# Outlook attention on one core: each landed band of coefficients is copied into pairs of heads before the banded matmuls

## The chip, the core and the metric

The kernel runs on one core of a Trainium2 chip. A core has a matrix engine (TensorE, PE in the profile, with its weight loads as PEld), a vector engine (VectorE, DVE), a scalar engine (ScalarE, ACT), GpSimd (POOL) and SyncE (SP), whose queue issues most of the DMAs. The engines run on their own and wait for one another through semaphores. The metric is the time of one execution on the device in microseconds; a kernel is run three times or more and the median is given. A profile is one further execution, recorded by the hardware.

## What is computed

The whole program is a two-layer network over x of shape 4 x 32 x 32 x 384: an attention, a mixture of experts, an outlook attention and a factored two-layer net, each added to x. The change lies in the outlook attention, whose reference is:

```python
def _L1_conv_ref(x, Wv, Wa, Wo):
    HEADS, K, PAD = (12, 3, 1)
    v = jnp.einsum('bhwc,oc->bhwo', x, Wv)
    ...
    v_unf = patches.reshape(b, n, k2, heads, d)
    a = jnp.einsum('bhwc,oc->bhwo', x, Wa).reshape(b, n, heads, k2, k2)
    attn = jax.nn.softmax(a * d ** (-0.5), axis=-1)
    out = jnp.einsum('bnhpq,bnqhd->bnphd', attn, v_unf).reshape(b, h, w, k2, c)
    ...
    for i in range(k):
        for j in range(k):
            canvas = canvas.at[:, i:i + h, j:j + w].add(out[:, :, :, p])
            p += 1
    y = canvas[:, pad:pad + h, pad:pad + w]
    return jnp.einsum('bhwc,oc->bhwo', y, Wo)
...
x = x + _L1_conv_ref(_ln_c(x), L1_conv_Wv, L1_conv_Wa, L1_conv_Wo)
```

Each pixel has, for each of 12 heads, a 9 x 9 matrix of softmax weights. It mixes the nine values around the pixel into nine outputs, which are added onto the nine pixels around it. Put together, an output pixel is a weighted sum over the values of a 5 x 5 neighbourhood, with one coefficient (a sum of softmax weights) per head and offset. In the order of rows of 32 pixels, those offsets reach 66 pixels back and forth.

## The kernel before

**Tiling.** The 4 images of 1024 pixels are 32 tiles of 128 pixels, eight to an image (`NB = 8`); a tile's number is `o = b * NB + t`. Everything is float32. All of the outlook layer is in the function `outlook` (L1764); it runs from about 2265 to 2730 us of the span, between the experts (`experts`) and the factored net (`Kron.run`).

**What is done for a tile.** Five functions, each called once a tile or half image:

- `scores(b, t)` (L1852): normalizes the tile (`xn`), transposes it on TensorE (`ps_tr`) and copies the result to `xnT` (ScalarE, L156), computes the logits `ps_a` with twelve matmul records (L1862, two PSUM banks, one buffer), takes maximum, difference (VectorE, L1871 and L1872), exponential (ScalarE, L1877), sums and the division (VectorE, L1879 to L1886), and sends rows of the result to neighbouring partitions by DMA into `up` and `down` (SP queue, L1898 to L1903). It then computes the values `ps_v` (L1906) and copies them to `v` (ScalarE, L1910).
- `band(b, t)` (L1912): adds up the shifted pieces in `u` (two ScalarE copies, L1919 and L1920, and three VectorE additions), shifts sideways with matmuls (`ps_c`, L1927), masks into `co` (L1935), and writes `co` to a DRAM buffer `room` (SP queue, L1942). The write has one row of 5 x 60 coefficients per pixel and the rows lie skewed, so that reading the buffer back with another row length (L1948) gives the tile `band` of 128 partitions x `BAND` = 260 columns x 12 heads: for each of 128 input pixels, the coefficients to the 260 output pixels around, and zeros between. This is one DMA of 1560 KB.
- `gather(b, half, t)` (L1953): the banded matmuls. For each head `h` it multiplies the 128 x 32 values of the head with the 128 x n coefficients of the head (n = 260, or 194 or 66 where the band is cut at the edge of a half image of 512 pixels), and adds into `ps_y`. Four heads lie side by side in four column tiles (32 output partitions each), so the twelve heads are three groups `c` of four. In the trace a float32 matmul leaves two records, so a gather has 24. Tiles 3 and 4 of an image are gathered twice, once for each half. After the last tile of a half, ScalarE copies the three banks to `y` (L1973).
- `mix(b, half, n, y)` (L1976): the output projection `ps_wo` (L1980) and the addition to x (L1984).
- `add(i)` (L1831): for the first 15 or so steps, adds experts' results (gathered by GpSimd's indirect DMA into `yt`) to tiles that later steps need.

**The coefficients of one head** are read by the matmul as `bands[b, t][:, j : j + hi - lo, h]`: in memory the 12 heads of a column lie next to each other, so consecutive columns of one head lie 12 floats apart.

**What sets the order.** A loop of steps (L2018) calls `scores` for tile `step`, then the functions that were put down for this step with `at`: `band` two steps after its tile's scores, `gathered` `LAG` = 3 steps after that, `mixed` later. SyncE and GpSimd issue in this written order (`manual_schedule`, L2279). For TensorE, VectorE and ScalarE the framework's list scheduler orders the instructions at build, by the written order as priority and by when it reckons operands and buffers to be ready; on the chip each engine then keeps that order. A pool with `bufs=n` gives n buffers to a tag, and a new tile waits until the instructions that use the old one are done. `reuse_waits="tile"` tells the framework to keep such waits by the tile.

Of the kernel before, what the change touches and what calls it, by code (L numbers as in the profile page):

```python
# [10 lines left out]
FP = mybir.dt.float32  # L11
# [6 lines left out]
P = 128  # L18
# [5 lines left out]
NH, HD = 12, 32  # L24
# [18 lines left out]
BAND = P + 2 * REACH  # L43
# [1720 lines left out]
def outlook(net, wv, wa, wo, left, router, kron, loads):  # L1764
# [10 lines left out]
    tc, nc = net.tc, net.nc  # L1775
    K2, H6 = 9, NH // 2
# [3 lines left out]
    with ExitStack() as ctx:  # L1780
# [2 lines left out]
        mp = ctx.enter_context(tc.tile_pool(name="ol_moved", bufs=4, reuse_waits="tile"))  # L1783
        ap_ = ctx.enter_context(tc.tile_pool(name="ol_attn", bufs=3, reuse_waits="tile"))
        vp = ctx.enter_context(tc.tile_pool(name="ol_v", bufs=7, reuse_waits="tile"))
        bp = ctx.enter_context(tc.tile_pool(name="ol_band", bufs=5, reuse_waits="tile"))
        ps_m = ctx.enter_context(tc.tile_pool(name="ol_ps_m", bufs=2, space=PSUM, reuse_waits="tile"))
        ps_a = ctx.enter_context(tc.tile_pool(name="ol_ps_a", bufs=1, space=PSUM, reuse_waits="tile"))
        ps_c = ctx.enter_context(tc.tile_pool(name="ol_ps_c", bufs=1, space=PSUM, reuse_waits="tile"))
# [4 lines left out]
        for dx in (-1, 0, 1):  # L1794
            m = const.tile([P, P], FP, name=f"shift_{dx}", tag=f"shift_{dx}")
# [41 lines left out]
                )  # L1837
            net.measure(work, i, net.x(i))

        attn, vs, bands, ys, moved = {}, {}, {}, {}, {}  # L1840

        def room(b, t):

# [68 lines left out]
        def band(b, t):  # L1912


            H3 = 3 * H6
            u = work.tile([P, 6, 5, H3], FP, name="u", tag="u")
            down, up = (m.rearrange("p (g y e) -> p g y e", g=6, y=3) for m in moved.pop((b, t)))
            own = attn.pop((b, t))[:, 1].rearrange("p s x (y e) -> p (s x) y e", y=3)
            nc.scalar.copy(u[:, :, 0, :], down[:, :, 0, :])  # L1919
            nc.scalar.copy(u[:, :, 4, :], up[:, :, 2, :])  # L1920
            nc.vector.tensor_tensor(u[:, :, 1:3, :], down[:, :, 1:3, :], own[:, :, 0:2, :], ALU.add)
            nc.vector.tensor_tensor(u[:, :, 3, :], own[:, :, 2, :], up[:, :, 1, :], ALU.add)
            nc.vector.tensor_tensor(u[:, :, 2, :], u[:, :, 2, :], up[:, :, 0, :], ALU.add)
            pc = ps_c.tile([P, 512], FP, name="ps_c", tag="c")
            grid = pc[:, : 5 * R].rearrange("p (s y e) -> p s y e", s=2, y=5)
            for qj in (1, 0, 2):
                nc.tensor.matmul(  # L1927
                    grid[:, :, :, (2 - qj) * H6 : (5 - qj) * H6],
                    lhsT=shift[qj - 1],
                    rhs=u.rearrange("p (s x) y e -> p s x y e", s=2)[:, :, qj, :, :],  # L1930
                    start=qj == 1, stop=qj == 2, skip_group_check=True,
                )
            co = work.tile([P, 5, 5, NH], FP, name="co", tag="co", bufs=3)
            for hh in range(2):
                nc.vector.tensor_tensor(  # L1935
                    co[:, :, :, hh * H6 : (hh + 1) * H6],
                    grid[:, hh].rearrange("p y (x h) -> p y x h", x=5),
                    inside.rearrange("p (x h) -> p x h", x=5).unsqueeze(1).to_broadcast([P, 5, 5, H6]),
                    ALU.mult,
                )  # L1940
            room = net.room[t]
            nc.sync.dma_start(  # L1942
                out=room.rearrange("(p r) -> p r", p=P)[:, : 5 * IMG * NH]
                .rearrange("p (y r) -> p y r", y=5)[:, :, :R],
                in_=co.rearrange("p y x h -> p y (x h)"),
            )
            m = bands[b, t] = bp.tile([P, BAND, NH], FP, name="band", tag="band")
            nc.sync.dma_start(  # L1948
                out=m.rearrange("p t h -> p (t h)"),
                in_=room[: P * BAND * NH].rearrange("(p r) -> p r", p=P),  # L1950
            )

        def gather(b, half, t):  # L1953

            first, last = (0, 4) if half == 0 else (3, 7)
            lo = max(P * t - REACH, 512 * half)
            hi = min(P * t - REACH + BAND, 512 * half + 512)
            j = lo - (P * t - REACH)
            for c in range(KC):
                if t == first:  # L1960
                    ys[c] = ps_y.tile([P, 512], FP, name=f"ps_y{c}", tag=f"y{c}")
                for n in range(4):
                    h = 4 * c + n
                    nc.tensor.matmul(  # L1964
                        ys[c][32 * n : 32 * n + 32, lo - 512 * half : hi - 512 * half],
                        lhsT=vs[b, t][:, h * HD : (h + 1) * HD],
                        rhs=bands[b, t][:, j : j + hi - lo, h],
                        start=t == first, stop=t == last, skip_group_check=True,
                    )
            if t == last:  # L1970
                y = work.tile([P, KC, 512], FP, name="y", tag="y", bufs=1)
                for c in range(KC):
                    nc.scalar.copy(y[:, c, :], ys[c])  # L1973
                return y
# [14 lines left out]
        def at(step, f, *args):  # L1989
            later.setdefault(step, []).append((f, args))  # L1990

        LAG = 3
        made = {}

        def gathered(b, half, t):
            y = gather(b, half, t)
            if y is not None:
                made[b, half] = y
# [4 lines left out]
        for b in range(B):  # L2003
            for t in range(NB):
                o = b * NB + t
                at(o + 2, band, b, t)
                at(o + 2 + LAG, gathered, b, 0 if t < 5 else 1, t)
                if t == 4:
                    at(o + 2 + LAG, gathered, b, 1, 3)
                    at(o + 2 + LAG, gathered, b, 1, 4)  # L2010
            for half in range(2):
                done = b * NB + (4 if half == 0 else 7) + 2 + LAG
                for n in range(4):
                    at(done + 1 + n // 2, mixed, b, half, n)
        assert left[0] >= 2 * NB
        t_kron, first = 0, left[0]
        for step in range(B * NB + 9):
            b, t = divmod(step, NB)  # L2018
# [207 lines left out]
def metaformer_kernel(  # L2226
# [19 lines left out]
    def rest(router, done):  # L2246

        with ExitStack() as late:
# [30 lines left out]
            with tc.manual_schedule(engines={eng.SP, eng.Pool}):  # L2279
                outlook(net, wv, wa, wo, range(done, NT), router, kron, loads)  # L2280
# [85 lines left out]
```

## Time and profile before

The median of three runs is 2829.91 us (2828.95 to 2830.11). The profiled execution took 2827.02 us, of which the recorded span is 2825.3 us; the mean granted TensorE clock was 0.959.

| engine | busy us | share of the span | instructions |
|---|---|---|---|
| PE | 2615.5 | 93% | 14703 |
| PEld | 1570.2 | 56% | 14703 |
| DVE | 1720.6 | 61% | 4382 |
| ACT | 1203.6 | 43% | 2023 |
| POOL | 413.8 | 15% | 501 |

The page cuts the span into 40 equal slices of 70.6 us; a digit is the busy share in tenths:

```profile
PE   6889998999999997687999999999999988999988
DVE  1377777677778787657245444655555566877742
ACT  3778777678768876312222212112112122122225
PEclk9999999999999998789999999999999999999999
```

The outlook layer lies in slices 33 to 39 (the last eight digits but one): TensorE at eight or nine tenths, VectorE between four and eight, ScalarE at one or two. The page's list of the costliest groups has few lines of this layer, ps_a (L1862, 384 records, 169.5 us busy) at their head; the layer's other matmuls are found by asking for the groups of that stretch alone. A busy time of a group is the time in which at least one of its records runs: four matmuls in four column tiles run side by side, so the busy time of `ps_y` is far below its count times its mean duration. A wait is put down to whatever came last by the profile.

Among the DMA issues of the stretch from 2260 to 2760 us are 32 of `band<-room` (1560 KB), 32 of `room<-co` (150 KB), 60 of `up<-attn` and 60 of `down<-attn`, and early in it the loads of x for the later images (two of 1536 KB, one of 1344 KB). They share one queue.

### The profile page before, as it was taken

The numbers are of one execution on the slowest core, as the hardware profiler recorded it, in microseconds if no ns is written. First come the engines' busy times: TensorE is split into PE (matmuls) and PEld (weight loads), VectorE is DVE, ScalarE is ACT, GpSimd is POOL, SyncE is SP. The second block draws the span as 40 slices with busy tenths as digits, with TensorE's granted clock in tenths as the row PEclk, the third lists the DMA queues.
The fourth block names the chain that finished last, engine by engine and source line by source line (L and its number), as shares of the span: only waits on it lengthen the run. The fifth ranks groups of instructions, "written<-read, shape, count | busy, mean of one in ns | idle before, by whom it ended". The sixth has DMA issues, their size and how long they took to land. (4 is left out here: it accounts for less than half of the span.)

```text
span 2825.3 us, 40024 instructions
## 1 busy us (share of the span) xinstructions
PE 2615.5 (93%) x14703; PEld 1570.2 (56%) x14703; DVE 1720.6 (61%) x4382; ACT 1203.6 (43%) x2023; POOL 413.8 (15%) x501
## 2 busy tenths in 40 slices
PE   6889998999999997687999999999999988999988
PEld 3323333333333332167899999999999944444432
DVE  1377777677778787657245444655555566877742
ACT  3778777678768876312222212112112122122225
POOL 1000000030003003213211112222221101100000
PEclk9999999999999998789999999999999999999999
DMA  5143434222323242453655455565665447554432
GB/s 106 31 106 90 110 92 129 75 66 72 90 60 75 68 108 58 125 204 125 248 229 208 167 208 209 210 230 210 217 224 203 156 148 217 173 178 149 147 109 91
DMA packets 215804, 404.11 MB, mean 143 GB/s; under 512 B 83344, under 2 KB 176848, under 8 KB 202544
## 3 DMA queue, kind: packets, MB, share of 16 engines
q1 hardware_dynamic: 184496, 187.82, 22.3%
q0 software_dynamic: 26960, 209.05, 21.5%
q10 hardware_dynamic: 4144, 4.61, 0.5%
q8 instruction: 118, 1.93, 0.3%
q14 instruction: 86, 0.70, 0.1%
HBM read 304.34 MB, written 49.00 MB: 125 GB/s over the span
## 5 line engine op out<-in xcount | busy, mean ns | idle before, releaser
L1698 ACT ACTIVATE h<-ps_h,up 128x256 f32<-128x256 f32 (+1 forms) x420 | 195.1, 465 | 839.7 <-PE ps_h L1693 838.8
L1693 PE MATMUL ps_h<-xbT,up 128*128 128x256 f32 (+1 forms) x2520 | 531.8, 372 | 2.5 <-ACT h L1698 1.8
L689 DVE CUSTOM_DVE_ANT_0 e<-e,rz,inv 128x1024 f32<-128x1024 f32 x384 | 475.2, 1274 | 44.6 <-DMA rz<-r_row 44.3
L1693 PEld LDWEIGHTS ps_h<-xbT,up 128*128 128x128 f32 x2520 | 463.1, 191 | 64.5 <-ACT h L1698 2.6
L637 ACT ACTIVATE e<-ps_s,ten 128x1024 f32<-128x1024 f32 x384 | 408.1, 1110 | 64.8 <-PE ps_s L627 33.1
L627 PE MATMUL ps_s<-q,k 32*128 32x512 f32 x1536 | 295.2, 673 | 44.7 <-ACT e L637 31.4
L645 PE MATMUL ps_o<-e,wv 128*32 128x512 f32 x1536 | 226.1, 663 | 50.9 <-DVE wv L696 49.4
L1735 PE MATMUL ps_y<-wsum,hsum 128*128 128x192 f32 x1152 | 205.4, 332 | 22.8 <-DVE hsum L1656 19.6
L645 PE MATMUL ps_z<-e,rt_ones 128*32 128x512 f32 x1536 | 218.3, 642 | 0.0
L716 POOL DMA_DIRECT2D q<-po x96 | 76.1, 877 | 951.5 <-DMA q<-po 560.9
L373 ACT ACTIVATE below<-tk_left,tk_bound 128x1024 bf16<-128x1024 f32 (+1 forms) x160 | 184.4, 1152 | 52.6 <-DVE tk_bound L379 40.4
L1735 PEld LDWEIGHTS ps_y<-wsum,hsum 128*128 128x128 f32 x1152 | 190.9, 193 | 27.3 <-DVE hsum L1656 21.3
L627 PEld LDWEIGHTS ps_s<-q,k 32*128 32x128 f32 x1536 | 92.5, 193 | 182.2 <-ACT e L637 90.2
L1862 PE MATMUL ps_a<-wa,xnT 128*128 128x486 f32 x384 | 169.5, 589 | 9.2 <-DVE attn L1872 7.5
L1739 DVE TENSOR_TENSOR y<-ps_y,y 128x192 f32<-128x192 f32 x160 | 57.2, 357 | 172.0 <-PE ps_y L1735 168.8
L645 PEld LDWEIGHTS ps_o<-e,wv 128*32 128x32 f32 x1536 | 31.4, 112 | 212.5 <-DVE wv L696 64.5
L288 PE MATMUL ps_t<-xnT,wqkv 128*128 128x512 f32 x288 | 135.1, 609 | 2.4 <-ACT xnT L470 1.7
L1735 PE MATMUL ps_y<-down,h 128*128 128x192 f32 x768 | 130.0, 326 | 0.0
L1735 PEld LDWEIGHTS ps_y<-down,h 128*128 128x128 f32 x768 | 126.6, 190 | 1.9
L1862 PEld LDWEIGHTS ps_a<-wa,xnT 128*128 128x128 f32 x384 | 72.3, 194 | 95.2 <-issue 85.5
L645 PEld LDWEIGHTS ps_z<-e,rt_ones 128*32 128x32 f32 x1536 | 52.2, 117 | 131.0 <-issue 127.5
L1540 POOL DMA_INDIRECT yt<-yg,index x64 | 76.7, 1198 | 323.0 <-DVE x L1835 135.3
(392 smaller groups left out, 3539.2 us busy)
## 6 DMA issues: line engine op xcount, KB each, us to landing
band<-room SPq DMA_DIRECT2D x32, 1560.0 KB
rz<-r_row SPq DMA_DIRECT2D x48, 512.0 KB
yg<-y SPq DMA_DIRECT2D x67, 192.0 KB
q<-q SPq DMA_DIRECT2D x192, 64.0 KB
k<-k SPq DMA_DIRECT2D x192, 64.0 KB
room<-none SPq DMA_DIRECT2D x64, 192.0 KB
x<-x SPq DMA_DIRECT2D x35, 192.0 KB
o<-in_x_dram SPq DMA_DIRECT2D x33, 192.0 KB
```

The costliest lines, as they stand in the source:

```text
L288: nc.tensor.matmul(ps, lhsT=lhsT(k), rhs=rhs(k), start=k == 0, stop=k == KC - 1)
L373: nc.scalar.activation(junk[:n], left[:n], AF.Sign, bias=bound[:n], accum_out=over[:n])
L627: nc.tensor.matmul(ps[:, half * 512 : half * 512 + 512], lhsT=self.k4[r, u * P : (u + 1) * P], rhs=self.q4[r, :], start=True, stop=True,)
L637: nc.scalar.activation(e, ps, AF.Exp, bias=shift, scale=QK_SCALE)
L645: nc.tensor.matmul(ps[r : r + 32, :], lhsT=lhsT(odd), rhs=self.es[2 * u + odd][:, half * 512 : half * 512 + 512], start=u == 0, stop=u == ...
L689: nc.vector.tensor_tensor_reduce(self.es[m], self.es[m], self.rz, 1.0, self.im["inv"][:, m, self.h : self.h + 1], ALU.mult, ALU.add, self. ...
L716: nc.gpsimd.dma_start(out=there, in_=po[r : r + 32, :], accum_op=ALU.add)
L1540: self.nc.gpsimd.indirect_dma_start(out=y, out_offset=None, in_=self.net.yg[: first_row(self.complete(i // NB)), :], in_offset=bass.Indire ...
L1693: nc.tensor.matmul(ps, lhsT=up[:, o : o + P], rhs=xbT[:, k, :size], start=k == 0, stop=k == KC - 1,)
L1698: nc.scalar.activation(hs[f // 3][:, f % 3, :size], ps, AF.Gelu, bias=up[:, KC * HID + f : KC * HID + f + 1])
L1735: nc.tensor.matmul(ps, lhsT=left[f], rhs=right[:, f, :], start=f == 0, stop=f == HF - 1)
L1862: nc.tensor.matmul(pa[:, hh, :HW_], lhsT=xnT[:, k, :], rhs=wa[:, k, hh * HW_ : (hh + 1) * HW_], start=k == 0, stop=k == KC - 1,)
```

## The change

The landed band isn't read by the matmuls any more. A new function `sort`, called one step before the gather of its tile, copies it with six ScalarE copies, one for each pair of heads, from the order (column, head) into a new tile `own` of the order (pair of heads, column, head of the pair). The matmul reads `own` with the head's pair and its place in it: consecutive columns of one head now lie 2 floats apart. The five buffers of `band` become three for the landed bands and two for `own`, of the same size each.

```diff
-        bp = ctx.enter_context(tc.tile_pool(name="ol_band", bufs=5, reuse_waits="tile"))
+        bp = ctx.enter_context(tc.tile_pool(name="ol_band", bufs=1, reuse_waits="tile"))
...
-        attn, vs, bands, ys, moved = {}, {}, {}, {}, {}
+        attn, vs, landed, bands, ys, moved = {}, {}, {}, {}, {}, {}
...
-            m = bands[b, t] = bp.tile([P, BAND, NH], FP, name="band", tag="band")
+            m = landed[b, t] = bp.tile([P, BAND, NH], FP, name="band", tag="band", bufs=3)
             nc.sync.dma_start(
                 out=m.rearrange("p t h -> p (t h)"),
                 in_=room[: P * BAND * NH].rearrange("(p r) -> p r", p=P),
             )
+
+        def sort(b, t):
+
+            m = landed.pop((b, t)).rearrange("p t (n h) -> p n t h", h=2)
+            own = bands[b, t] = bp.tile([P, H6, BAND, 2], FP, name="own", tag="own", bufs=2)
+            for n in range(H6):
+                nc.scalar.copy(own[:, n], m[:, n])
...
-                        rhs=bands[b, t][:, j : j + hi - lo, h],
+                        rhs=bands[b, t][:, h // 2, j : j + hi - lo, h % 2],
...
                 at(o + 2, band, b, t)
+                at(o + 1 + LAG, sort, b, t)
                 at(o + 2 + LAG, gathered, b, 0 if t < 5 else 1, t)
```

In the list of a step, the entries stand by tile: the gather of tile `step - 5` first, then `sort` of tile `step - 4`, then `band` of tile `step - 2`.

## The prediction

> **What bounds the kernel now.** I read the page first (the row of busy tenths shows TensorE at nine tenths in slices 35 to 38), then the busy time of each engine stage by stage, then the groups of one stage by shape, then waits and order of time. The stage that the change touches runs from about 2265 to 2730 us of the span. By stretches:
>
> ```profile
> core 0: us, PE busy (x) PEld busy (x) DVE busy (x) ACT busy (x) POOL busy (x), PEclk, DMA share, GB/s
> 2320.00:2345.00 25.00, 24.38 (x103) 11.34 (x103) 17.07 (x42) 4.82 (x12) 2.49 (x3) 0.94 0.75 244
> 2345.00:2420.00 75.00, 64.30 (x310) 30.93 (x309) 53.49 (x138) 13.84 (x27) 14.81 (x15) 0.91 0.61 187
> 2420.00:2690.00 270.00, 268.79 (x1221) 132.44 (x1220) 198.05 (x502) 61.46 (x121) 12.05 (x15) 1.00 0.50 163
> 2710.00:2730.00 20.00, 12.34 (x83) 4.44 (x82) 3.89 (x10) 3.04 (x4) 0.00 (x0) 0.83 0.48 169
> ```
>
> In 2420 to 2690 TensorE is busy 268.8 of 270 us, VectorE 73%, ScalarE 23%; and what TensorE waited for there adds up to 1.2 us:
>
> ```profile
> PE ps_a L1862 <- ACT xnT L156: 0.6, 1, 0.6
> PE ps_c L1927 <- DVE u L1923: 0.4, 1, 0.4
> PE ps_a L1862 <- DVE attn L1872: 0.2, 1, 0.2
> ```
>
> So TensorE alone bounds these 270 us at full granted clock. Before 2420 it idles 14% behind other waits (DMA landings); after 2710 a chain of DMAs ends last. The banded matmuls there (each a pair of records, four column tiles side by side, so mean durations overlap; busy time is what counts):
>
> ```profile
> L1964 PE MATMUL ps_y<-band,v 128*32 128x260 f32 x226 | 35.5, 627 | 0.0
> L1964 PE MATMUL ps_y<-band,v 128*32 128x194 f32 x240 | 26.4, 515 | 0.0
> L1964 PE MATMUL ps_y<-band,v 128*32 128x66 f32 x96 | 3.6, 295 | 0.0
> ```
>
> 65.5 us, a quarter of the stage.
>
> **Edit 1: the matmul's moving operand (L1967) goes from a step of 12 floats (48 bytes) to 2 floats (8 bytes).** Start to start is the true pace, since ends are modelled. In order of time:
>
> ```profile
> 517.55 1.07 PE L645 MATMUL ps_o<-e,wv 128*32 128x512 f32 x8
> 518.43 1.04 PE L645 MATMUL ps_z<-e,rt_ones 128*32 128x512 f32 x8
> ...
> 2428.20 2.22 PE L1964 MATMUL ps_y<-band,v 128*32 128x194 f32 x24
> 2430.35 0.91 PE L1906 MATMUL ps_v<-wv,xnT 128*128 128x384 f32 x2
> ...
> 2458.15 2.90 PE L1964 MATMUL ps_y<-band,v 128*32 128x260 f32 x24
> 2460.99 0.55 PE L155 MATMUL ps_tr<-ident,xn 128*128 128x128 f32 x3
> ```
>
> 24 records are three groups of four heads, two passes each: six passes. 260 columns: 2.84/6 = 0.473 us a pass; 194 columns: 2.15/6 = 0.358 us. The slope is 0.115/66 = 1.74 ns a column, the rest 0.02 us; 66 columns (0.82/6 = 0.137 us) lie on the same line. The attention's ps_o runs in the same four column tiles, with contiguous operands: 0.88 us for two passes of 512, 0.86 ns a column. So four tiles side by side are not what costs; the step is, by a factor of 2.0.
>
> No matmul of this trace steps by 8 bytes, so its price lies between 0.86 and 1.74 ns. [...] That saves 48%, 48% and 44%: of 35.5, 26.4 and 3.6 us **17.1 + 12.6 + 1.6 = 31 us** in the bound stage. From 2320 to 2420 the same matmuls are 20.8 us busy and lose 10, but TensorE isn't alone in setting the time there: I count 3.
>
> **Edit 2: `sort`, six ScalarE copies a band, 6 x 32 = 192**, each 128x520, read in runs of two floats 48 bytes apart, written contiguously. Rows of ScalarE:
>
> ```profile
> L1877 ACT ACTIVATE attn<-attn 128x972 f32<-128x972 f32 x20 | 20.3, 1015 | 12.1 <-DVE attn L1872 12.1
> L1920 ACT COPY u<-up 128x108 f32<-128x108 f32 x21 | 6.0, 284 | 9.8 <-DMA up<-attn 9.7
> ...
> 2697.16 1.56 ACT L1973 COPY y<-ps_y 128x512 f32<-128x512 f32 x3 [3.72 <-PE ps_y L1964]
> ```
>
> Between 108 and 972 elements the slope is 0.85 ns, so 520 elements take 284 + 412 x 0.85 = 633 ns; the three y copies in a row (mean 590) start 0.49 us apart, so I take 0.53 us apiece in a row: 3.2 us a band, 102 us in all. [...] The lower end is the 3.2: the contiguous row leaves no room for less. About 21 bands fall into the bound stage: ScalarE goes from 61 to 128 us busy, of some 245. It has the room; its cover is idle time now spent waiting for ps_v, ps_tr and the DMAs of `down`. Were it full, each copy would cost its 0.53 us.
>
> **Edit 3: the new waits.** A copy waits for its band to land and for one of two `own` buffers, freed by the gather two tiles before. The band is no problem in steady state: its DMA is issued at 2507.49, the next two runs of ps_a begin at 2515.00 and 2530.70, `sort` comes with the second, and in the drain such a DMA needs 6.2 us. The buffer is free a step before it is wanted, except at tile 3 of each image, kept for two gathers: four places. Queued behind a copy on ScalarE are xnT (ps_a waits for it), the exponential (VectorE waits, then the DMAs of `up` and `down`), v, and the u copies.
>
> [...] If a whole batch stood ahead of xnT in each step, ps_a would wait 3.2 us less what still covers it. Today 1.91 us of ps_y cover it (ps_y starts 2513.09, xnT is done at 2513.68, ps_a starts 2515.00); halved, about 1.0 us, of which 0.6 is used: 0.4 us left, so up to 2.8 us x 21 steps = 59 us lost. By the trace, ScalarE is idle 77% of the stage, its order is chosen at build, and the copies are six pieces that can run long before their gather; so usually one piece of 0.6 us stands ahead, about half the time: 0.2 to 0.3 us a step, up to 6 us; I take 4. VectorE becomes 198/245 = 81% busy, and waits for it that today cost 0.6 us will show: I take 4 us.
>
> **Edit 4: buffers.** Landed bands have 3 instead of 5; a buffer is freed by `sort`, a step earlier than by the gather. The SP queue could stop on it only if `sort` fell over a step behind: 0. The memory is the same, (3 + 2) bands.
>
> **The end.** The last band lands at about 2724.9, then gather (2.2 us), y copies, ps_wo. Now 3.2 us of copies come first and a gather of 1.1 us follows, partly beside them: +2 us. TensorE does nothing else then; no cover.
>
> **Sum** against the profiled 2827.0 us (span 2825.3 plus 1.7 around it): -31 - 3 + 4 + 4 + 2 = -24, so 2803. The runs' median lies 2.9 us above the profiled one: **2806 us**. As forecast its own range is 2790 to 2818: the lower end keeps all 41 us less 2, the upper one some half of the gain.
>
> **Rivals.**
> - *The next bound takes most of it.* VectorE's chain a_max, attn, exponential, rows, and the DMAs of `up` and `down` behind it, would end last. For it: 73% busy, and in 2345 to 2420, at the same 71%, TensorE already idles. Against: 1.2 us of waits in 270. A third of the 31 stays: -10 + 2 = 2822.
> - *ScalarE's queue makes it slower.* Place: the six copies ahead of xnT and the exponential. It decides from 31/21 = 1.5 us of stall a step; with the whole batch ahead (59 us) the time is 2830 - 31 + 59 + 2 = 2860, with two thirds of it 2840. For it: xnT's thin cover, and the waits of ScalarE for other engines (v 63.6, u 56.3, xnT 51.3 us) with which a copy may now be late. Against: the idle 77%.
> - *An 8-byte step is as slow as a 48-byte one*, so the change doesn't do what it says: gain 0, end +2, small stalls up to 8: 2832 to 2840. For it: no row. [...]
>
> **Chances.** Forecast 0.55, next bound 0.17, ScalarE's queue 0.18, step still slow 0.10. The smallest change that this measurement tells from none is about 0.2%, 5.7 us. Faster: nearly all of the first two, 0.69. Same: parts of the last three near 2830, 0.08. Slower: the third and half of the last, 0.23. The range must hold 2840 and part of the queue's case: 2790 to 2846, leaving some 0.06 below and 0.1 above.
>
> **What would show it.** Right: 24 records of 260 columns start to start in about 1.5 us; ps_y's busy time in the stage near 34 us; 192 copies of 500 to 650 ns; TensorE still over 93% busy; the stage's 270 us now some 245. [...]

## The result, and the profile after

The changed kernel takes 2810.77 us (median of four runs, 2808.80 to 2812.25) against 2830.01 us: ratio 0.9924, 95% interval 0.9910 to 0.9939. That is 19 us faster; 2806 was forecast. Its profiled execution took 2811.76 us, span 2809.9, which is 15.4 us less span than before. The layer itself, from its first exponential to the end of the span, lost 19.7 us (546.9 to 527.2); it began 4.3 us later, after work that the change doesn't touch (in the profile of the repeated change it began at 2278.7 us, against 2278.4 before).

From the page after, engine totals and the line of the new copies:

```profile
PE 2585.7 (92%) x14703; PEld 1567.7 (56%) x14703; DVE 1722.3 (61%) x4382; ACT 1309.9 (47%) x2215; POOL 411.9 (15%) x501
L1958 ACT COPY own<-band 128x520 f32<-128x520 f32 x192 | 111.3, 658 | 60.4 <-DMA band<-room 57.1
```

TensorE lost 30 us of busy time, ScalarE gained 106. The banded matmuls by shape, in the layer's stretch of the changed kernel:

```profile
L1971 PE MATMUL ps_y<-own,v 128*32 128x260 f32 x384 | 35.4, 399 | 3.5 <-ACT own L1958 3.4
L1971 PE MATMUL ps_y<-own,v 128*32 128x194 f32 x384 | 27.4, 355 | 4.0 <-ACT own L1958 4.0
L1971 PE MATMUL ps_y<-own,v 128*32 128x66 f32 x192 | 7.4, 239 | 2.6 <-ACT own L1958 2.4
```

Together 70.2 us; before, over all of the layer, the three shapes had 55.0, 41.4 and 8.6 us, 105.0 in all. So 35 us of matmul time are gone and 20 us of it reached the end.

To see where the other 15 stayed, I take the 32 exponentials (L1877), one for each tile's scores, as marks and cut the layer at the 5th, the 18th and the last (tiles 4, 17 and 31). Busy time by stretch, before and then after (the first two rows of each are tiles 4 to 17); columns are the stretch, its length, busy time (and instructions) of each engine, granted clock, share of the DMA engines, GB/s:

```profile
2319.60:2388.80 69.20, 61.14 (x298) 29.22 (x299) 46.26 (x114) 12.16 (x28) 13.07 (x14) 0.90 0.67 214
2388.80:2496.80 108.00, 103.86 (x495) 51.56 (x494) 87.02 (x221) 26.56 (x52) 15.19 (x16) 0.98 0.59 185
2496.80:2692.40 195.60, 195.18 (x852) 95.21 (x855) 137.84 (x348) 42.28 (x83) 1.08 (x3) 1.00 0.47 155
```

```profile
2324.50:2378.20 53.70, 49.12 (x278) 24.96 (x282) 43.47 (x108) 27.88 (x54) 10.52 (x12) 0.97 0.77 244
2378.20:2500.40 122.20, 105.11 (x551) 56.01 (x542) 90.80 (x232) 57.37 (x108) 15.94 (x18) 0.93 0.60 179
2500.40:2676.30 175.90, 173.20 (x829) 92.23 (x829) 137.25 (x345) 88.77 (x169) 1.08 (x3) 1.00 0.51 168
```

The last row of each (tiles 17 to 31) is 19.7 us shorter, 1.4 a tile, with TensorE full before and after. It also holds fewer matmul records after (829 against 852): the order that the build chose for TensorE has changed, and some 3 us of work now stand before the mark, as the old-step run below shows. In the first two rows TensorE's busy time falls from 165.0 to 154.2 us, but its idle time grows from 12.2 to 21.7: the sum goes from 177.2 only to 175.9. These are the steps in which `add` runs. TensorE's waits there after, then VectorE's longest after and before (us, times, longest):

```profile
PE ps_a L1862 <- DVE attn L1872: 8.9, 3, 4.7
PE ps_tr L155 <- DVE x L1991: 7.8, 1, 7.8
```

```profile
DVE x L1835 <- DMA yt<-yg,index: 22.7, 11, 4.4
```

```profile
DVE x L1835 <- DMA yt<-yg,index: 17.0, 8, 5.0
```

TensorE waits for VectorE, and VectorE stands at `add` (L1835) until GpSimd's gather of `yt` has landed. GpSimd in turn cannot begin a gather before VectorE is done with a buffer of `yt`; what GpSimd waited for most there, after:

```profile
POOL yt L1540 <- DVE x L1835: 78.0, 15, 16.5
```

That is the suspect; the other is ScalarE's queue with the copies in it.

### The profile page after: what moved, and what is told of

The parts are those of the page before. It is cut to its first block, busy times and chain, and to the rows that moved or that the text cites. A ratio compares the mean times of both kernels' runs of the same rounds, so it can differ in the third digit from the quotient of the medians.

```text
span 2809.9 us, 40231 instructions
## 1 busy us (share of the span) xinstructions
PE 2585.7 (92%) x14703; PEld 1567.7 (56%) x14703; DVE 1722.3 (61%) x4382; ACT 1309.9 (47%) x2215; POOL 411.9 (15%) x501
## 3 DMA queue, kind: packets, MB, share of 16 engines
q1 hardware_dynamic: 184496, 187.82, 22.7%
q0 software_dynamic: 26960, 209.05, 21.7%
q8 instruction: 118, 1.93, 0.3%
## 5 line engine op out<-in xcount | busy, mean ns | idle before, releaser
L1698 ACT ACTIVATE h<-ps_h,up 128x256 f32<-128x256 f32 (+1 forms) x420 | 195.2, 465 | 839.6 <-PE ps_h L1693 836.1
L1958 ACT COPY own<-band 128x520 f32<-128x520 f32 x192 | 111.3, 658 | 60.4 <-DMA band<-room 57.1
```

Of the source, the lines that this page charges most:

```text
L1698: nc.scalar.activation(hs[f // 3][:, f % 3, :size], ps, AF.Gelu, bias=up[:, KC * HID + f : KC * HID + f + 1])
L1958: nc.scalar.copy(own[:, n], m[:, n])
```

## The experiments

Runs were made on different chips. On one of them (old step, quads, singles, and the change with 4 yt buffers) the kernel before took 2875 us, so ratios and the layer's own times are compared, not absolute times. Each row's stretches are of one profiled execution: that of old step took 6 us and that of singles 9 us more than the median of its runs, that of the repeated change 6 us less. A few us between rows therefore count only where the ratios agree. The stretches are between the marks above; "end" is from the last exponential to the end of the span.

| kernel | ratio to before (95%) | tiles 0-4 | 4-17 | 17-31 | end | layer |
|---|---|---|---|---|---|---|
| before | | 41.1 | 177.2 | 195.6 | 132.9 | 546.9 |
| the change | 0.9924 (0.9910-0.9939) | 41.8 | 175.8 | 175.9 | 133.6 | 527.2 |
| the change again | 0.9948 (0.9932-0.9963) | 42.0 | 175.0 | 176.3 | 134.5 | 527.7 |
| old step | 1.0014 (1.0002-1.0026) | 41.9 | 180.4 | 192.2 | 136.1 | 550.6 |
| quads | 1.0029 (1.0019-1.0039) | 42.9 | 187.1 | 192.3 | 136.0 | 558.3 |
| triples | 1.0005 (0.9992-1.0019) | 42.6 | 182.9 | 183.7 | 134.1 | 543.4 |
| singles | 1.0000 (0.9988-1.0012) | 42.2 | 189.7 | 185.5 | 137.3 | 554.7 |
| change, 4 yt buffers | 0.9866 (0.9839-0.9894) | 39.5 | 158.4 | 175.5 | 134.2 | 507.5 |
| before, 4 yt buffers | 0.9957 (0.9939-0.9976) | 37.5 | 164.4 | 196.0 | 134.3 | 532.2 |
| change, 4 yt, drain in place | 0.9849 (0.9826-0.9872) | 37.8 | 159.7 | 175.8 | 134.7 | 508.1 |

**The copies alone (old step).** The copy keeps the old order:

```diff
-            own = bands[b, t] = bp.tile([P, H6, BAND, 2], FP, name="own", tag="own", bufs=2)
+            own = bands[b, t] = bp.tile([P, BAND, NH], FP, name="own", tag="own", bufs=2)
             for n in range(H6):
-                nc.scalar.copy(own[:, n], m[:, n])
+                nc.scalar.copy(own.rearrange("p t (n h) -> p n t h", h=2)[:, n], m[:, n])
...
-                        rhs=bands[b, t][:, h // 2, j : j + hi - lo, h % 2],
+                        rhs=bands[b, t][:, j : j + hi - lo, h],
```

> The six copies, their waits and their buffers as in the change, but the copy keeps the old order (column, head), so that the matmuls step by 48 bytes as before. Line theory (the matmul's pace is set by hits on a 16-byte line): 24 records of 260 columns take 2.84 us again, ps_y 1.74 ns a column. On what the copies cost by themselves: in the changed kernel's steps 0 to 9 and 17 to 31 TensorE gained 1.4 us a step, in steps 9 to 17 it lost 14 us. Queue theory (the 14 us are copies standing in ScalarE's queue): they are lost here too, about 2830 + 14 + 2 for the end = 2846 us. Next-bound theory (VectorE and the gathers of yt hold TensorE once it is faster): with TensorE as slow as before nothing is lost there, about 2832 us.

The matmuls are as slow as before (the piece of work shown below takes 1.90 us in both). The median is 4.5 us (0.6 to 7.5) above that of the kernel before on the same chip, and the layer takes 3.7 us more: 192 copies with all their waits cost about 4 us, not 14 and more. Tiles 4 to 17 take 180.4 us, within 5 us of both other kernels, whether the matmuls are fast or slow. So the queue theory fails here; that something else paces these steps also when the matmuls are fast is shown by the runs with more buffers for yt. Tiles 4 to 17, then 17 to 31, of this run:

```profile
2374.90:2555.40 180.50, 168.14 (x808) 81.10 (x812) 134.59 (x339) 85.53 (x161) 26.82 (x30) 0.97 0.63 193
2555.40:2747.60 192.20, 192.20 (x839) 93.89 (x834) 137.40 (x345) 89.82 (x168) 1.08 (x3) 1.00 0.47 156
```

With matmuls of the old pace TensorE is busy 3 us less than before in the last stretch (192.2 against 195.2) and 3 us more in the one ahead (168.1 against 165.0): this is the work that changed sides of the mark. Of the change's 19.7 us in tiles 17 to 31, some 3 are thus moved work and 16 to 17 the faster matmuls; and its 1.4 us in tiles 4 to 17 were gained with 3 us more work in them.

**What sets the matmul's pace: quads, triples, singles.** The same copy with other groups of heads; for quads

```diff
-            m = landed.pop((b, t)).rearrange("p t (n h) -> p n t h", h=2)
-            own = bands[b, t] = bp.tile([P, H6, BAND, 2], FP, name="own", tag="own", bufs=2)
-            for n in range(H6):
+            m = landed.pop((b, t)).rearrange("p t (n h) -> p n t h", h=4)
+            own = bands[b, t] = bp.tile([P, NH // 4, BAND, 4], FP, name="own", tag="own", bufs=2)
+            for n in range(NH // 4):
                 nc.scalar.copy(own[:, n], m[:, n])
...
-                        rhs=bands[b, t][:, h // 2, j : j + hi - lo, h % 2],
+                        rhs=bands[b, t][:, h // 4, j : j + hi - lo, h % 4],
```

(triples with 3 for 4), and for singles

```diff
-            m = landed.pop((b, t)).rearrange("p t (n h) -> p n t h", h=2)
-            own = bands[b, t] = bp.tile([P, H6, BAND, 2], FP, name="own", tag="own", bufs=2)
+            m = landed.pop((b, t)).rearrange("p t (n h) -> p n h t", h=2)
+            own = bands[b, t] = bp.tile([P, H6, 2, BAND], FP, name="own", tag="own", bufs=2)
...
-                        rhs=bands[b, t][:, h // 2, j : j + hi - lo, h % 2],
+                        rhs=bands[b, t][:, h // 2, h % 2, j : j + hi - lo],
```

> Three copies of four heads side by side: a matmul's step is 16 bytes, one hit on each 16-byte line. Line theory: the matmul is as slow as with 48 bytes, 2.84 us for 24 records of 260 columns, and the time is back at 2830 to 2846 us. Rival (the pace grows with the distance of the step): 16 bytes lie near 8, about 1.5 to 1.8 us for 24 records, and the time stays near 2811 us. The copies, 128x1040 each in runs of 16 bytes, take about 284 + 932 x 0.85 = 1.08 us each by both.

> Four copies of three heads side by side: a step of 12 bytes, three columns on every four floats, so 1.33 hits on a line on average. If a line costs 1.7 ns however many of its floats are used, the pace is 3/4 of that, 1.25 to 1.3 ns a column, about 2.1 us for 24 records of 260 columns. If a matmul needs two hits on every line or falls to the slow pace as a whole, 2.84 us.

> The six copies write each head contiguously, so that the matmul steps by 4 bytes and the copy reads single floats 48 bytes apart. Line theory: the matmul stays at 1.5 us for 24 records of 260 columns (two hits suffice, four add nothing), and the copy, with one hit a line, slows like the matmul did, from 0.66 to about 1.1 us (520 elements at 1.7 ns in place of 0.85, plus the same 0.19), ScalarE some 80 us busier. Rival (the line matters to TensorE only): copies of 0.66 us. The time: 2811 us if ScalarE has the room still, up to 2830 us if its queue begins to hold TensorE.

The comparison needs the same piece of work: part of a gather, 10 records, with the start of ps_a behind it. These are five heads: four side by side in two passes, then one alone in two, so four passes of 260 columns one after the other. In order of time, start and length in us; singles (4-byte step), then the change (8), triples (12), quads (16), the kernel before (48):

```profile
2519.84 1.06 PE L1971 MATMUL ps_y<-own,v 128*32 128x260 f32 x10
2520.83 0.68 PE L1862 MATMUL ps_a<-wa,xnT 128*128 128x486 f32 x1
```

```profile
2514.68 1.11 PE L1971 MATMUL ps_y<-own,v 128*32 128x260 f32 x10
2515.72 0.68 PE L1862 MATMUL ps_a<-wa,xnT 128*128 128x486 f32 x1
```

```profile
2521.70 1.56 PE L1971 MATMUL ps_y<-own,v 128*32 128x260 f32 x10
2523.18 0.68 PE L1862 MATMUL ps_a<-wa,xnT 128*128 128x486 f32 x1
```

```profile
2511.87 2.00 PE L1971 MATMUL ps_y<-own,v 128*32 128x260 f32 x10
2513.80 0.68 PE L1862 MATMUL ps_a<-wa,xnT 128*128 128x486 f32 x1
```

```profile
2555.88 1.97 PE L1964 MATMUL ps_y<-band,v 128*32 128x260 f32 x10
2557.78 1.08 PE L1862 MATMUL ps_a<-wa,xnT 128*128 128x486 f32 x2
```

Start to start: 0.99, 1.04, 1.48, 1.93 and 1.90 us. Less 0.02 us a pass and divided by 4 x 260 columns that is 0.88, 0.92, 1.35, 1.78 and 1.75 ns a column. The old-step run has 1.90 us as well. The last pass of a piece also holds the change to ps_a; between the starts of the third and the fourth pass alone lie 0.22, 0.23, 0.34, 0.46 and 0.45 us, or 0.84, 0.88, 1.32, 1.77 and 1.74 ns a column. A step of 16 bytes is as slow as one of 48 (1.77 and 1.74 ns), so between these two the distance doesn't matter, and triples lie between pairs and quads. Counted in lines of 16 bytes, the columns per line are 4, 2, 1.33, 1 and 1; at 1.33 and 1 the measured times come to 1.74 to 1.77 ns a line (triples: 1.32 ns a column, three quarters of a line), and at 2 and 4 the matmul runs at 0.88 and 0.84 ns a column, near the 0.86 of ps_o, whose operands are contiguous. The runs show these paces, not what makes them. (Triples were expected at 1.25 to 1.3, just below. That quads and triples also take 7 to 11 us more than the change in tiles 4 to 17 was not followed up.)

The price shifts to ScalarE. Copies of singles, then of quads:

```profile
L1958 ACT COPY own<-band 128x520 f32<-128x520 f32 x192 | 199.7, 1120 | 38.2 <-DMA band<-room 33.8 <-PE ps_c L1927 4.3
```

```profile
L1958 ACT COPY own<-band 128x1040 f32<-128x1040 f32 x96 | 95.8, 1057 | 55.5 <-DMA band<-room 51.4 <-PE ps_y L1971 4.1
```

Reading single floats 48 bytes apart, a copy of 520 elements takes 1120 ns against 658 in pairs. With matmuls as fast as any, singles gain nothing (ratio 1.0000, where the change has 0.9924 and 0.9948): 88 us more of ScalarE cost the whole gain, in the rows some 14 us in tiles 4 to 17, 10 in 17 to 31 and 4 at the end, though these rows are of an execution 9 us longer than the median. This is the queue rival of the prediction at 1.7 times the copy's price (1120 against 658 ns); it ends level with before, at the upper end of what was expected. Of the four groupings pairs alone came out faster than before: the matmul at 0.88 ns a column with copies of 658 ns for 520 elements.

**The bound of the early steps: more buffers for yt.**

```diff
-                y = bp.tile([P, C], FP, name="yt", tag="yt", bufs=2)
+                y = bp.tile([P, C], FP, name="yt", tag="yt", bufs=4)
```

> The changed kernel with four buffers instead of two for yt, the tile into which GpSimd gathers the experts' results for add. Next-bound theory (in steps 9 to 17 VectorE stands at add, which waits for the DMA of yt, and with it all that is queued behind): the waits of VectorE for yt shrink from some 30 us to under 10, and 8 to 14 us are gained: 2797 to 2803 us. Queue theory: the loss lies with ScalarE's copies, nothing changes, 2811 us.

> The kernel before, with four buffers instead of two for yt and nothing of the change. If steps 4 to 17 are paced by add's gathers and TensorE's pace sets the rest: VectorE's waits for yt vanish here too, but TensorE has only 11 us of idle time between 2320 and 2420 to lose and is full afterwards, so at most 11 us are gained, ratio 0.996 to 0.999; steps 17 to 31 stay at 195 us, against 175 in the changed kernel. If more buffers for yt are worth what they were on top of the change (about 17 us up to step 17), the ratio is 0.994 or less and the two gains are independent.

The two gathers that a tile needs take two buffers; with four, those of the next tile can start before VectorE is done with them. On top of the change, tiles 4 to 17 fall by 17 us to 158.4 (8 to 14 were expected), the ratio to 0.9866. The two stretches of that run, and VectorE's wait for yt in them:

```profile
2366.80:2422.80 56.00, 49.85 (x282) 25.33 (x284) 43.92 (x109) 28.10 (x55) 13.03 (x15) 0.97 0.79 246
2422.80:2525.10 102.30, 99.98 (x551) 53.66 (x542) 89.36 (x231) 57.05 (x106) 13.83 (x15) 1.00 0.69 207
```

```profile
DVE x L1835 <- DMA yt<-yg,index: 0.2, 1, 0.2
```

The wait is gone (0.2 us instead of 22.7), and TensorE idles 8.5 us instead of 21.7; the copies are all there, 46 us of ScalarE busy time more than before the change, so it isn't their queue that held these steps. Another 4.4 us of the 17 are TensorE's busy time, 149.8 instead of 154.2 for nearly the same work: in the second row the granted clock is 1.00 instead of 0.93. In the kernel before, the same edit gives less: 12.8 us in these steps, ratio 0.9957 or 12 us, a little over the 11 expected, since TensorE is soon full (103.3 us busy of the last 105.0 up to tile 17, 195.2 of 196.0 behind it). With yt out of the way the layer takes 532.2 us without the change and 507.5 with it: the change is then worth 24.7 us instead of 19.7. Ratios of one chip agree: the change alone gives 15 us (0.9948), the buffers alone 13 (0.9957), both with the in-place reading described below 41 (0.9849), more than the sum.

**The change again** was run on the chip of the runs with triples, before with 4 yt buffers, and drain in place:

> The changed kernel as it is, on the same chip as the other three, so that they can be compared with it: ratio to the kernel before 0.992, as measured, by each theory.

0.9948 (0.9932 to 0.9963) overlaps the first measurement at its edge; both say faster.

**The end.** On top of four yt buffers, the last three bands are read in place:

```diff
             m = landed.pop((b, t)).rearrange("p t (n h) -> p n t h", h=2)
+            if b * NB + t >= B * NB - 3:
+                bands[b, t] = m
+                return
```

> The change with four buffers for yt, and the last three bands not copied but read in place with a step of 48 bytes: after the last scores TensorE has little to do, and the copies lie on the chain of the last DMAs. If the copies cost 1 to 2 us at the end: the time from the last exponential to the end of the span falls from 133.6 to about 132 us; all before is as in the run with four yt buffers, ratio 0.986. If the end is set by the DMAs alone, it stays at 133.6.

From the last gather's start, or its copies', to ps_wo it takes 2.2 us, as in the kernel before, instead of 4.3; but the last band landed later after the last exponential (33.3 us, against 31.3 in the change and 32.5 before), and the end as a whole is 134.7 us, no shorter. The ratio 0.9849 can't be told from 0.9866. So the 2 us are real at their place, and whether they reach the end stays open.

## Why the prediction was right, point by point

- **TensorE alone bounds 2420 to 2690.** Right for tiles 17 to 31, where nearly all of the gain fell and TensorE is busy 173.2 of 175.9 us after; wrong for the first 77 us of the stage, up to tile 17 (below).
- **The 8-byte step costs what contiguous data cost.** Right: 24 records of 260 columns now take 1.51 us, 0.252 us a pass, and 194 columns 1.17 us, 0.195; at ps_o's 0.86 ns a column and 0.02 us a pass it would be 0.244 and 0.187. No run had shown a step of 8 bytes when the sum was made: that its 31 us (and the 3 before 2420) could be counted at the contiguous pace was the author's estimate. The changed kernel then showed 0.88 ns a column at 8 bytes, triples 1.32 at 12 and quads 1.77 at 16, so the time of a column doubled between 8 and 16 bytes. In the tally of busy time 35 us are saved; 31 in the bound stage and 10 before it were forecast, some 6 too much. A gather that runs in one go does save 47 and 46% of its time (48 forecast), so most of the 6 are lost in gathers that are cut into pieces, wait for a copy midway (one of 24 records took 2.86 us) or run at a lowered clock (0.93 granted from 2378.2 to 2500.4 us); how they divide was not followed up.
- **The copies: 3.2 us a band, hidden.** They take 3.48 us a band, 111 us in all instead of 102 (658 ns apiece, just above the 650 named as a sign), and the old-step run shows that they cost about 4 us, the end included.
- **The losses: 4 us for xnT, 4 for VectorE, 2 at the end.** TensorE's waits for xnT rose from 6.8 to 9.4 us: 2.6. In tiles 17 to 31 VectorE cost nothing to speak of: TensorE's idle time there rose only from 0.4 to 2.7 us, where about 6 of the 8 us were due. That this part of the sum came out is partly luck: by the faster pace TensorE's busy time fell there by 19 us (22.0, less the 3 that moved), where the forecast's share is 22, and the two errors cancel. The end came out 0.7 us longer (1.6 in the repetition).
- **The stretch before 2420: 3 us.** This is where the sum was off. In tiles 4 to 17 the banded matmuls' busy time fell by 14.0 us (39.0 to 25.0), some 3 us of work moved in, and 9.5 us came back as idle time. I had seen that TensorE wasn't alone there, but let the bound stage begin at 2420, where the trace of before turned full; once the matmuls were faster, `add` paced up to tile 17, some 80 us longer. The rival of the next bound was thus partly true, with another bound than the one named: not VectorE's chain of maximum and exponential, nor the DMAs of `up` and `down`, but VectorE standing in line behind two buffers of yt. The waits of ps_a for attn and of ps_c for u, where VectorE's chain would have shown, stood at 13.0 us over the layer, hardly above the 11.5 before; the largest new wait was another, 7.8 us of ps_tr for x (L1991). Nor had the sum a term for the granted clock: over the 122.2 us up to tile 17, where TensorE idled 17.1 us, it was 0.93, and with four yt buffers, at 2.3 us of idle time in the same work, 1.00 (last section).
- **ScalarE's queue.** Not at the price that pairs have; it takes the whole gain at the price of singles.

The best version that was run is the change with four buffers for yt: ratio 0.9866, about 38 us; the change alone gave 19 and, repeated, 15, the buffers alone 13. The one that also reads the last bands in place (0.9849) is not distinguishable from it.

## What to carry to other kernels

When a matmul's operand steps through memory, compare it start to start with a contiguous matmul of the same column tiles, and try the small steps: here 8 bytes ran at the contiguous pace (0.88 against 0.84 ns a column), 12 bytes at 1.32 and 16 bytes, like 48, at 1.74 to 1.77. Count what the copy that makes the order costs too: reading pairs of floats it took 658 ns for 520 elements, reading single ones 1120, and the dearer copy used up the matmuls' gain. A stage's bound holds only as long as what fills it is slow: before counting a gain up to a certain time, ask which small waits lie hidden in the stretch (here 17 us of VectorE for yt) and what they will cost when the cover is gone. Such a wait may go for a few kilobytes of buffers (here two more of 1.5 KB a partition).

## What the runs showed of the hardware that wasn't expected

ScalarE's copies here took longer with short runs on reading and not on writing. Over a copy of 108 elements (284 ns), pairs cost (658 - 284)/412 = 0.91 ns a float, singles 2.03, triples 1.05, quads 0.83; the old-step run writes its pairs 48 bytes apart and takes 656 ns, the same as contiguous writing.

With more idle time on TensorE these runs also show a lower granted clock and slower matmuls. In the changed kernel, after the longest wait of ps_a, in order of time, and then the row of busy times of the same stretch, whose third figure from the end is the granted clock:

```profile
2486.27 1.96 PE L1862 MATMUL ps_a<-wa,xnT 128*128 128x486 f32 x2 [4.68 <-DVE attn L1872]
2488.02 0.81 PE L1927 MATMUL ps_c<-u,shift 128*128 128x180 f32 x2
```

```profile
2486.20:2490.00 3.80, 3.73 (x9) 2.81 (x10) 2.04 (x9) 3.43 (x7) 0.00 (x0) 0.50 0.62 187
```

Two records of ps_a take 1.75 us start to start, where they take 0.8 otherwise, and a pair of ps_c records shows 0.81 us instead of 0.47. The wait of 4.7 us was followed by matmuls at half pace, with a granted clock of 0.50; it is 0.82 from 2490 to 2494 and 1.00 again from 2494 to 2498. Over tiles 4 to 17 TensorE's busy time fell together with its idle time: with four buffers for yt nearly the same work took 4.4 us less of it in the changed kernel, as said above, and 4.7 us less in the kernel before (165.0 to 160.3, with a granted clock of 1.00 instead of 0.95).
